# A transformer step on one core: the first mixture of experts gets its whole issue order written out, with all norms ahead, the gates of three chunks in one chain, and the rotary angles and the first attention block spread over the pairs

## The chip, the cores and the metric

The kernel runs on one core of one Trainium2 chip, as a single launch. The metric is the device time of that launch in microseconds. Before the change it is 1956.31 us, the median of three runs (1955.98 to 1956.78).

The core has five engines with a queue of instructions each: TensorE (PE) multiplies matrices, VectorE (DVE), ScalarE (ACT) and GpSimd (POOL) do the elementwise work, and SyncE (SP) issues the transfers between memory and the on-chip buffers. Every engine works its queue in order. Where an instruction waits for another engine, everything behind it on its own engine waits too.

## The reference

A batch of 2 sequences of 1024 tokens with 128 channels goes through six steps. The change touches the first and the beginning of the second:

```
x = x + 0.5 * L0_ffn(layernorm(x))        # mixture of experts: the "first mixture"
x = x + L0_attn(layernorm(x))             # attention, 16 heads of 64, over 1024 tokens
x = x + 0.5 * L0_ffn(layernorm(x))        # the same mixture again
x = x + 0.5 * L1_ffn(layernorm(x))        # two layers of local attention and gated MLP
x = x + L1_attn(layernorm(x))             # linear attention
x = x + 0.5 * L1_ffn(layernorm(x))

def L0_ffn(xf):                           # 16 experts of width 64, one shared expert of width 128
    shared = silu(xf @ Sg) * (xf @ Su) @ Sd
    probs  = softmax(xf @ Wr)             # 16 values for each token
    cw     = probs where it is one of the two largest, else 0
    routed = sum over e of cw[:, e] * (silu(xf @ Wg[e]) * (xf @ Wu[e]) @ Wd[e])
    return routed + shared

def L0_attn(x):
    q, k, v = heads of x @ qkv_w.T
    ang = pos[:, None] * rope_freqs       # q and k are rotated by cos(ang), sin(ang)
    scores = q @ k.T / 8 - p * log1p(a * abs(i - j))      # p, a: one number for each head
    return softmax(scores) @ v @ out_w.T
```

The routing is computed densely: every expert sees every token, and the weight `cw` sets most of the products to zero.

## The kernel before, in words

Everything is float32. `x` stays on chip as 16 tiles of 128 tokens by 128 channels. The kernel is built in Python; a loop in it is unrolled into instructions.

**The mixture** (`mixture`, L195) works on four chunks of 512 tokens. For each chunk there is a *front*. It has 13 parts (`front_parts`, L274): five for the norm (statistics on DVE, a negated mean on POOL, Ln and Exp on ACT, the offset on POOL, and four normalises on ACT, `norm_pieces`, L147), a transpose of four tiles on PE (`front_turned`), its copy by ACT (`front_kept`, into `xnT`), the logits on PE (`front_logits`), four parts for the gates (`front_gates`, L225: softmax and the two largest of 16, some twenty small operations on DVE and one Exp on ACT), and `front_weights` (L262), which transposes the weights on PE, copies them by DVE and stores them in DRAM.

After that come nine *pairs* for each chunk: first the shared expert (number `NP` = 8), then eight pairs of experts. A pair consists of

- `entered` (L294): the gate and up matmuls into one of two double banks of the accumulator memory,
- `fetched` (L303): two transfers of a row of weights from DRAM, repeated over 64 partitions (`cb`),
- `gated` (L310): silu on ACT; `multiplied` (L318): the product with `up` on DVE; `weighted` (L322): the product with `cb` on POOL (not for the shared expert),
- `left` (L326): the down matmuls, which add into `acc`. `finish` (L344) adds half of `acc` to `x`, on DVE.

**What is done beside the pairs.** `run_moe` (L350) walks over chunks and pairs and calls `prepare` (L455) after each pair. After the second pair of chunk 0 that emits `tables` (L413): the loads of the query and key weights and their scaling on POOL, the distances `dist`, and the rotary angles: sixteen DVE operations on 128x1024 that reduce the angle into the range of the sine, then Sin and Abs on ACT. In chunk 1 it emits the four bias pieces for the heads of pairs 0 and 1 (`bias_part`: Ln on ACT and a multiply on DVE, 128x1920). After chunk 1 and after chunk 3 it emits the attention's norm and transposes for one batch (`norm_transposed`, L177). In chunks 2 and 3 it emits the twelve *units* of the first attention block (`block_of`, L485): eight `rotary` units (one matmul each; two DVE products each; after every second one two POOL sums and eight small transfers into `qk`) and four `values` units.

**What sets the order.** In the first mixture the order in which Python emits is only a proposal: the framework's scheduler places the instructions of each engine by its own estimate. So the gate operations of chunk 1 stand between the angle operations on DVE, and the scores of the first attention step come ahead of the last down matmul on PE. In the attention (L657) and in the later stages the order is written out by hand (`tc.manual_schedule()`), and the queues hold what Python emits.

**The attention** runs 128 steps, one for each group of heads, batch, pair of heads and tile of 128 queries. Each takes scores (`scores_of`), the sum with the bias and its extremum on DVE (`maxima`, L558), Exp on ACT, a scaling on POOL, transposes, and, two to four steps later, the product with the values. The next block's units and the next pairs' bias pieces (L671 to L674) go beside the steps.

**Queues and buffers that the change touches.** SP issues all transfers in order, and a ninth waits for the completion of the first of the last eight. The double bank of `entered` has two buffers, `h` three, `cb` four, `xnT` two.

Of the kernel before, what the change touches and what calls it, by code (L numbers as in the profile page):

```python
# [8 lines left out]
F32 = mybir.dt.float32  # L9
# [22 lines left out]
def macaron_kernel(ctx: ExitStack, tc: tile.TileContext, a: dict, out: bass.AP):  # L32
# [41 lines left out]
    for i in range(4):  # L74
        nc.sync.dma_start(out=x[:, 4 * i : 4 * i + 4, :], in_=xv[:, 4 * i : 4 * i + 4, :])

    wr = keep.tile([P, E], F32, name="wr")
    nc.sync.dma_start(out=wr, in_=a["L0_ffn_Wr"])
# [6 lines left out]
    nc.sync.dma_start(out=wg, in_=a["L0_ffn_Wg"].rearrange("e p f -> p e f"))  # L85
    nc.sync.dma_start(out=wu, in_=a["L0_ffn_Wu"].rearrange("e p f -> p e f"))
    nc.sync.dma_start(out=wd, in_=a["L0_ffn_Wd"].rearrange("(i e) f m -> (e f) i m", e=2))
    nc.sync.dma_start(out=sg, in_=a["L0_ffn_Sg"])
    nc.sync.dma_start(out=su, in_=a["L0_ffn_Su"])
    nc.sync.dma_start(out=sd, in_=a["L0_ffn_Sd"])  # L90

# [23 lines left out]
    def norm_stats(src, n, name):  # L115

        st = small.tile([P, TB, 6], F32, tag="st", name=f"st_{name}")
        mv = small.tile([P, TB, 2], F32, tag="mv", name=f"mv_{name}")
        for i in range(n):
            nc.vector.bn_stats(st[:, i, :], src[:, i, :])  # L120
            nc.vector.bn_aggr(mv[:, i, :], st[:, i, :])
        rs = small.tile([P, TB], F32, tag="rs", name=f"rs_{name}")
        nc.scalar.activation(rs[:, :n], mv[:, :n, 1], AF.Ln, bias=eps)
        nc.scalar.activation(rs[:, :n], rs[:, :n], AF.Exp, scale=-0.5)
        nb = small.tile([P, TB], F32, tag="nb", name=f"nb_{name}")
        nc.gpsimd.tensor_scalar(nb[:, :n], mv[:, :n, 0], -1.0, 1.0, ALU.mult, ALU.mult)
        nc.gpsimd.tensor_tensor(nb[:, :n], nb[:, :n], rs[:, :n], ALU.mult)
        return rs, nb

# [8 lines left out]
    def log_and_exp(ins):  # L138

        with tc.issue_after(ins.ins):  # L140
            nc.scalar.preload_act_table_set("natural_log_exp_and_others")

    def normalise(dst, src, stats, k):
        rs, nb = stats
        nc.scalar.activation(dst, src, AF.Identity, bias=nb[:, k : k + 1], scale=rs[:, k : k + 1])

    def norm_pieces(src, n, name, dst):  # L147

        st = small.tile([P, TB, 6], F32, tag="st", name=f"st_{name}")
        mv = small.tile([P, TB, 2], F32, tag="mv", name=f"mv_{name}")  # L150
# [1431 lines left out]
```

## Time and profile before

| | us |
|---|---|
| median of 3 runs | 1956.31 |
| the profiled execution | 1957.24 |
| its span, first to last instruction | 1955.5 |
| PE busy in the span | 1841.8 (94%) |
| DVE, ACT, POOL busy | 1393.9, 1164.9, 1126.0 |
| first instruction of PE | 13.69 |
| first gate matmul of the mixture | 17.82 |
| end of the last down matmul of the first mixture | 164.72 |
| first score sum of attention step 2 on DVE | 183.39 |

The span and the busy times come from the page of the profile, the positions from the timeline of the instructions, counted from the first instruction. How the page is read: a group of the same instructions has one line, with the tile it writes, an arrow, the tiles it reads, their shapes, the count, the busy time and the mean of one; after the bar stands the idle time of that engine just before them, and who ended it. A matmul in float32 appears as two instructions. PE's granted clock is given as a share of full speed.

The first mixture and the ramp of the attention take the first tenth of the span. The rest (attention, second mixture, local and linear attention) runs with PE above 80% in every slice but the last.

### The profile page before, as it was taken

The numbers are of one execution on the slowest core, as the hardware profiler recorded it, in microseconds if no ns is written. First come the engines' busy times: TensorE is split into PE (matmuls) and PEld (weight loads), VectorE is DVE, ScalarE is ACT, GpSimd is POOL, SyncE is SP. The second block draws the span as 40 slices with busy tenths as digits, with TensorE's granted clock in tenths as the row PEclk, the third lists the DMA queues.
The fourth block names the chain that finished last, engine by engine and source line by source line (L and its number), as shares of the span: only waits on it lengthen the run. The fifth ranks groups of instructions, "written<-read, shape, count | busy, mean of one in ns | idle before, by whom it ended". The sixth has DMA issues, their size and how long they took to land.

```text
span 1955.5 us, 37604 instructions
## 1 busy us (share of the span) xinstructions
PE 1841.8 (94%) x14460; PEld 1176.5 (60%) x14460; DVE 1393.9 (71%) x2466; ACT 1164.9 (60%) x2132; POOL 1126.0 (58%) x1028
## 2 busy tenths in 40 slices
PE   4998999999999999999999988999999899999997
PEld 2554666656665665656566556666656466666665
DVE  6555767786777767776763468788877888887883
ACT  6344555665566555665655456776666566677674
POOL 2344434354444435344444379888877788788883
PEclk8998999999999999999999999999999999999999
DMA  5221101010000101012013211111100000011111
GB/s 134 76 80 41 34 1 34 12 31 14 22 23 12 33 12 34 2 32 70 1 67 89 74 28 29 25 24 25 26 18 15 6 18 18 20 26 23 26 32 27
DMA packets 52415, 64.15 MB, mean 33 GB/s; under 512 B 17890, under 2 KB 26892, under 8 KB 51980
## 3 DMA queue, kind: packets, MB, share of 16 engines
q1 hardware_dynamic: 52236, 61.74, 12.4%
q8 instruction: 115, 1.88, 0.4%
q14 instruction: 64, 0.52, 0.1%
HBM read 27.89 MB, written 1.31 MB: 15 GB/s over the span
## 4 chain that ended last, share of the span: by engine, by line
PE 62%; DVE 13%; ACT 10%; issue 7%; POOL 6%; SPq 1%; DMA 1%; DVEq 0%; POOLq 0%; ACTq 0%
PE s L549 11%; PE tp L599 10%; PE av L616 9%; PE qk_f L877 4%; ACT p L578 3%; PE pq L497 2%; PE av_f L1049 2%; PE gu_m L300 2%; PE gu_m L301 2%; PE tq_f L944 2%; PE s_f L988 2%; PE tp_f L1035 2%; PE pj_f L1065 2%; PE acc_m L284 2%; PE v_f L955 2%
## 5 line engine op out<-in xcount | busy, mean ns | idle before, releaser
L585 POOL TENSOR_SCALAR p<-p,den 128x1024 f32<-128x1024 f32 x256 | 291.9, 1153 | 396.5 <-DVE den L583 312.8
L578 ACT ACTIVATE p<-p,nm 128x1024 f32<-128x1024 f32 x256 | 294.7, 1151 | 364.7 <-DVE nm L565 348.4
L565 DVE CUSTOM_DVE_ANT_0 p<-s,bias 128x1024 f32<-128x1024 f32 x256 | 302.9, 1220 | 110.4 <-PE s L549 109.1
L599 PE MATMUL tp<-ident,p 128*128 128x128 f32 x2048 | 275.3, 277 | 13.5 <-ACT pt L603 12.7
L599 PEld LDWEIGHTS tp<-ident,p 128*128 128x128 f32 x2048 | 225.6, 141 | 100.8 <-ACT pt L603 37.5
L549 PE MATMUL s<-qk,qk 64*128 64x512 f32 x1024 | 257.8, 618 | 0.3 <-DVE nm L565 0.3
L616 PE MATMUL av<-pt,v 128*64 128x256 f32 x2048 | 249.0, 385 | 0.0
L605 DVE COPY pt<-tp 128x512 f32<-128x512 f32 x256 | 176.3, 689 | 93.9 <-PE tp L599 93.6
L616 PEld LDWEIGHTS av<-pt,v 128*64 128x64 f32 x2048 | 135.8, 136 | 150.1 <-issue 83.7
L923 POOL TENSOR_TENSOR t_f<-t_f,t_f 128x1024 f32<-128x1024 f32 x64 | 151.3, 2365 | 31.1 <-ACT vo_f L966 20.1
L324 POOL TENSOR_TENSOR h_m<-h_m,cb_m 128x512 f32<-128x512 f32 x64 | 81.8, 1282 | 124.8 <-DVE h_m L320 108.4
L603 ACT COPY pt<-tp 128x512 f32<-128x512 f32 x256 | 147.6, 577 | 5.9 <-PE tp L599 5.9
L549 PEld LDWEIGHTS s<-qk,qk 64*128 64x128 f32 x1024 | 89.1, 187 | 84.1 <-issue 81.5
L890 ACT ACTIVATE t_f<-qk_f 128x1024 f32<-128x1024 f32 x64 | 65.5, 1024 | 111.2 <-PE qk_f L877 103.0
L898 DVE TENSOR_TENSOR t_f<-qk_f,tab 128x1024 f32<-128x1024 f32 x64 | 78.3, 1224 | 74.1 <-ACT t_f L890 74.1
L1027 POOL TENSOR_TENSOR s_f<-s_f,sm_f 128x1024 f32<-128x1024 f32 x64 | 121.5, 1899 | 9.9 <-DVE sm_f L1023 9.8
L877 PE MATMUL qk_f<-wqkv,hT 128*128 128x512 f32 x256 | 121.7, 598 | 5.0 <-DVE hT L871 1.9
L1013 POOL TENSOR_TENSOR s_f<-s_f,mx_f 128x1024 f32<-128x1024 f32 x64 | 123.9, 1935 | 0.4 <-DVE mx_f L1008 0.4
L928 POOL TENSOR_TENSOR t_f<-t_f,rn_f 128x1024 f32<-128x1024 f32 x64 | 122.0, 1905 | 0.2
L320 DVE TENSOR_TENSOR h_m<-h_m,gu_m 128x512 f32<-128x512 f32 x72 | 49.2, 686 | 89.4 <-ACT h_m L316 89.2
L316 ACT ACTIVATE h_m<-gu_m 128x512 f32<-128x512 f32 x72 | 42.9, 597 | 115.5 <-PE gu_m L301 108.0
L513 POOL TENSOR_TENSOR rot<-rot,rot 128x512 f32<-128x512 f32 x32 | 40.7, 1273 | 88.1 <-DVE rot L508 88.1
(380 smaller groups left out, 3783.8 us busy)
## 6 DMA issues: line engine op xcount, KB each, us to landing
cb_m<-cwd_m SPq DMA_DIRECT2D x128, 128.0 KB, 3.0
qk<-rot SPq DMA_DIRECT2D x256, 64.0 KB, 2.0
tab<-in_xpos_dram SPq DMA_DIRECT2D x2, 1024.0 KB
wqkv<-in_L_ffn_wqkv_dram SPq DMA_DIRECT2D x2, 768.0 KB, 8.3
x<-in_L_attn_x_dram SPq DMA_DIRECT2D x4, 256.0 KB, 3.0
wraw<-in_qkv_wT_dram SPq DMA_DIRECT2D x2, 512.0 KB
vb_f<-vo_f SPq DMA_DIRECT2D x8, 128.0 KB, 2.5
out_dram<-x SPq DMA_DIRECT2D x4, 256.0 KB, 2.3
```

The costliest lines, as they stand in the source:

```text
L549: nc.tensor.matmul(pss[r][:, c, :], lhsT=qT[rows[r], t * P : (t + 1) * P], rhs=kT[rows[r], c * 512 : (c + 1) * 512], start=True, stop=True,)
L565: nc.vector.tensor_tensor_reduce(out=s, in0=pss[r].rearrange("p a n -> p (a n)"), in1=bias[r][:, o : o + S], scale=-1.0, scalar=3.0e38, op ...
L578: nc.scalar.activation(s, s, AF.Exp, bias=nm[:, r : r + 1], scale=-1.0, accum_out=den[:, r : r + 1])
L585: nc.gpsimd.tensor_scalar(probs[i, r], probs[i, r], den[:, r : r + 1], 1.0, ALU.mult, ALU.mult)
L599: nc.tensor.transpose(tp[:, k * P : (k + 1) * P], s[:, kb * P : (kb + 1) * P], ident)
L603: nc.scalar.copy(dst, src)
L605: nc.vector.tensor_copy(dst, src)
L616: nc.tensor.matmul(po[r * 64 : r * 64 + 64, 0 : 2 * P], lhsT=v[:, kb, r * 64 : r * 64 + 64], rhs=pts[i // 2, r, g][:, kb - 4 * g, :], star ...
L877: nc.tensor.matmul(ps[:, s, :], lhsT=hTs[b][:, n * P : (n + 1) * P], rhs=lw[l][0][:, s * INNER : (s + 1) * INNER], start=True, stop=True,)
L923: nc.gpsimd.tensor_tensor(t1, t1, t2, ALU.add)
L928: nc.gpsimd.tensor_tensor(t3, t3, rn.unsqueeze(2).to_broadcast([P, 2 * HL, 64]), ALU.mult)
L1013: nc.gpsimd.tensor_tensor(s3, s3, mx.unsqueeze(2).to_broadcast([P, HL, P]), ALU.subtract)
```

## The change

The scheduler no longer places the first mixture: `first_mixture` writes the order of all engines out.

- **Loads.** `x` still comes first, with `wr` behind its first quarter; then `sg`, `su`, `wg`, `wu`, `sd`, `wd`. The loads of `wv` and `wo` move from the start into slots 6 and 10, those of the query and key weights into slots 2 and 8 (a slot is one pair of one chunk, 36 in all).
- **Norms and gates.** The statistics of all 16 tiles are taken before the first pair; chunk 0 is normalised on ACT, chunks 1 to 3 on POOL from one Ln and one Exp. The logits of chunks 1 to 3 go into one bank, and their gates run as one chain on 12 tiles. `xnT` has four buffers, `cb` and `h` five.
- **Slots.** In slot s come `entered`, `gated`, `multiplied` and `weighted` of slot s, then `left` of slot s - 3, then what is listed beside the slot, then `fetched` of slot s + 3. Beside the slots: `front_weights` of chunks 1, 2, 3 at 4, 8, 12; one angle operation in each of the slots 4 to 19, computed in place in `sinT` and `cosT`; Abs and Sin at 20 and 21; batch 0's norm at 12, 21 and 22, with the normalises on DVE; the units of block 0 in slots 23 to 34; the bias of pair 0 in four halves at 35.
- **Activation tables.** They are switched explicitly (`log_exp_set`, `silu_set`).
- **Attention.** The norm of batch 1 is split: half of its statistics at slot 30, the rest and the first normalises at slot 38, the transposes at steps 0 and 1. The bias of pair 1 moves into steps 3, 4, 5 and 7.

```diff
-    for i in range(4):
-        nc.sync.dma_start(out=x[:, 4 * i : 4 * i + 4, :], in_=xv[:, 4 * i : 4 * i + 4, :])
...
+    for i in range(4):
+        nc.sync.dma_start(out=x[:, 4 * i : 4 * i + 4, :], in_=xv[:, 4 * i : 4 * i + 4, :])
+        if i == 0:
+            nc.sync.dma_start(out=wr, in_=a["L0_ffn_Wr"])
...
+    def silu_set():
+        if written[-1] != "silu":
+            nc.scalar.preload_act_table_set("silu_and_others")
+            written.append("silu")
...
-    def run_moe(name, beside):
...
-            def tables(mp):
...
+            def angles(mp):
+                ang, kk = sinT, cosT
...
+                def cosine():
+                    nc.scalar.activation(cosT, ang, AF.Abs)
+                    silu_set()
+                    nc.scalar.activation(cosT, cosT, AF.Sin, bias=halfpi, scale=-1.0)
+                def sine():
+                    silu_set()
+                    nc.scalar.activation(ang, ang, AF.Sin)
+                return ops, cosine, sine
+            def norm_of_batch(b):
...
+                mo, ne, ro, of_, ap = norm_pieces(src, TB, f"a0{b}", xas, nc.vector)
...
+            def first_mixture(mp):
+                LAG = 3
+                fronts, left, finish, front_parts, pair_parts = mixture("m0", mp, cbs=5, hs=5, cws=2, xts=4)
...
+                mo0, ne0, ro0, of0, ap0 = norm_pieces(x[:, 0:4, :], 4, "m00", x0)
+                mo1, ne1, ro1, of1, ap1 = norm_pieces(x[:, 4:NT, :], 12, "m01", x1, nc.gpsimd, mp)
+                for fn in (mo0, ne0, ro0, of0, mo1, ap0):
+                    fn()
+                fronts[0] = (x0,)
+                turned_(0)
+                for fn in (ne1, ro1, of1):
+                    fn()
+                kept(0)
+                logits(0)
...
+                apply1(1)
+                gates(0, 0)
+                gates(0, 1)
+                lg = bankO("lg_m01", 0).rearrange("p (t e) -> p t e", e=E)[:, :12, :]
+                for c in range(1, 4):
+                    fronts[c] = (x1[4 * c - 4 : 4 * c],)
+                    turned_(c)
+                    if c < 3:
+                        apply1(c + 1)
+                    kept(c)
+                    logits(c, lg, 4 * c - 4)
+                fronts[1] = lg
+                gates(0, 2)
+                gates(1, 0, 12)
+                gates(1, 1, 12)
+                gates(0, 3)
+                silu_set()
+                entered(*slots[0])
+                entered(*slots[1])
...
+                at(0, weights, 0)
+                for s in (1, 2):
+                    at(0, fetched, *slots[s])
+                at(0, gates, 1, 2, 12)
+                at(2, gates, 1, 3, 12)
+                for c, s in ((1, 4), (2, 8), (3, 12)):
+                    at(s, lambda c=c: weights(c, fronts[1][2], 4 * c - 4))
+                load, scaled = query_weights(mp)
+                for s, at_load, at_scale in ((0, 2, 7), (1, 8, 12)):
+                    at(at_load, load, s)
+                    for u in range(2):
+                        at(at_scale + u, scaled, s, u)
...
+                at(5, nc.scalar.activation, dist, dist, AF.Abs)
+                at(6, lambda: nc.sync.dma_start(out=wv, in_=qw[:, 2 * n : 3 * n]))
+                at(10, lambda: nc.sync.dma_start(out=wo, in_=a["out_wT"].rearrange("(j p) m -> p j m", p=P)))
+                for k, op in enumerate(ops):
+                    at(4 + k, op)
+                at(4 + len(ops), cosine)
+                at(5 + len(ops), sine)
+                mo, ne, ro, of_, ap, up = norm_of_batch(0)
+                at(12, mo, range(4))
+                at(21, mo, range(4, TB))
+                for fn in (ne, ro, of_, silu_set):
+                    at(21, fn)
+                at(22, ap, 0)
+                at(22, up, 0)
+                at(22, ap, 1)
+                at(23, up, 1)
+                for u in range(12):
+                    at(23 + u, lambda u=u: blocks[0][2].pop(6 - 2 * (u // 3) if u % 3 == 2 else 0)())
+                mo, ne, ro, of_, ap2, up2 = norm_of_batch(1)
+                at(30, mo, range(4))
+                at(35, log_exp_set)
+                for k in range(4):
+                    at(35, bias_part, 0, k // 2, slice(k % 2 * WIDE // 2, (k % 2 + 1) * WIDE // 2))
+                for fn, *more in ((mo, range(4, TB)), (ne,), (ro,), (of_,), (ap2, 0)):
+                    at(38, fn, *more)
+                for s in range(len(slots) + LAG):
+                    if s < len(slots):
+                        if s > 1:
+                            entered(*slots[s])
+                        gated(*slots[s])
+                        multiplied(*slots[s])
+                        if slots[s][1] < NP:
+                            weighted(*slots[s])
+                    if s >= LAG:
+                        left(*slots[s - LAG])
+                        if slots[s - LAG][1] == NP - 1:
+                            finish(slots[s - LAG][0])
+                    for fn in beside.pop(s, ()):
+                        fn()
+                    if s + 3 < len(slots) and slots[s + 3][1] < NP:
+                        fetched(*slots[s + 3])
+                return ap2, up2
...
-            run_moe("m0", prepare)
+            with ExitStack() as ms, tc.manual_schedule():
+                ap2, up2 = first_mixture(pool("moe_m0", 3, ms, side="right", reuse_waits="tile"))
...
-                            if (b, j) == js and t in places and (hg + 1 < H0 // 4 if b else hg > 0):
+                            if (b, j) == js and t in places and (hg + 1 < H0 // 4 or not b):
...
+                    elif i == 0:
+                        up2(0)
+                        ap2(1)
                     elif i < len(steps):
+                        if i == 1:
+                            up2(1)
```

Behind attention step 14 the order of every engine's work is the same as before.

## The prediction

> **What bounds the kernel now.** I read the summary first: TensorE (PE) is busy 94% of the span and is the bound nearly everywhere, so a change gains only where PE stands idle or runs slowly. The table of stages says where that is.
>
> ```profile
> 0.00:16.00 16.00, 1.64 (x4) 0.73 (x4) 3.33 (x24) 10.86 (x19) 3.73 (x19) 1.00 0.99 230
> 16.00:30.00 14.00, 13.56 (x48) 7.96 (x48) 7.53 (x26) 9.23 (x14) 3.21 (x5) 1.00 0.41 122
> 30.00:170.00 140.00, 113.39 (x508) 67.61 (x508) 78.96 (x174) 59.40 (x85) 53.14 (x46) 0.95 0.25 73
> ```
>
> Columns: window, length, then PE, weight load, VectorE (DVE), ScalarE (ACT), GpSimd (POOL) busy, granted PE clock, DMA share, GB/s. Before 16 us PE waits for loads and norms; from 30 to 170 it is idle 26.6 us, and the clock is not always full. The timeline of PE shows the rest.
>
> ```profile
> 17.82 2.06 PE L300 MATMUL gu_m<-xnT_m,sg 128*128 128x512 f32 x2
> ...
> 32.29 2.08 PE L300 MATMUL gu_m<-xnT_m,wg 128*128 128x512 f32 x2 [2.64 <-DVE h_m L320]
> ...
> 49.57 2.07 PE L300 MATMUL gu_m<-xnT_m,wg 128*128 128x512 f32 x2 [11.90 <-DVE h_m L320]
> ...
> 59.49 1.02 PE L300 MATMUL gu_m<-xnT_m,wg 128*128 128x512 f32 x2
> 60.35 1.02 PE L301 MATMUL gu_m<-xnT_m,wu 128*128 128x512 f32 x2
> 61.21 1.05 PE L284 MATMUL acc_m<-wd,h_m 128*128 128x128 f32 x8
> 62.10 1.02 PE L300 MATMUL gu_m<-xnT_m,wg 128*128 128x512 f32 x2
> ...
> 163.56 1.16 PE L284 MATMUL acc_m<-wd,h_m 128*128 128x128 f32 x8 [0.22 <-POOL h_m L324]
> ...
> 171.32 2.40 PE L188 MATMUL tp_a<-ident,xn_a 128*128 128x128 f32 x6 [5.54 <-ACT xn_a L145]
> ```
>
> By the starts, a warm pair costs 0.86 + 0.86 + 0.89 = 2.61 us of PE. After a gap of 2.64 us or more the same matmul takes 2.07 instead of 1.02: the clock has fallen. The 11.90 us gap has its cause on DVE, in its timeline:
>
> ```profile
> 43.36 0.69 DVE L445 TENSOR_SCALAR kk<-ang 128x1024 f32<-128x1024 f32 x1
> 44.10 0.68 DVE L446 TENSOR_SCALAR kk<-kk 128x1024 f32<-128x1024 f32 x1
> ...
> 45.57 1.22 DVE L449 SCALAR_TENSOR_TENSOR ang<-kk,ang 128x1024 f32<-128x1024 f32 x1
> ...
> 48.84 0.68 DVE L320 TENSOR_TENSOR h_m<-h_m,gu_m 128x512 f32<-128x512 f32 x1
> ```
>
> Sixteen angle operations and the gates of chunk 1 run as one block, and the product that PE waits for stands behind them. The chain of waits says the same: issue on DVE for 15.12 us at 34.44.
>
> **The change, part by part.** A slot is one pair of one chunk, 36 in all. I follow the changed issue order of each engine with durations of these rows.
>
> *The front moves ahead.* Loads: x0 stays first, so the first norm still starts at 3.81. The two iotas (1.73, 0.98) go ahead of POOL's first norm work, hidden by the wait for x (done near 4.4). Statistics 1.2, Ln 0.29, Exp 0.20, offset 0.20, four normalises of 0.40: 7.5. Then the new waits: ACT's copy of chunk 0 stands behind Ln and Exp of the other twelve tiles, which wait for x3 and 24 DVE statistics, about 9.3 (12 x 0.21 and 12 x 0.09). Ln, Exp 9.9; copy 0.56; cold logits 1.89: 12.4. Chunks 1 to 3 follow one by one on PE and ACT: transposes 0.9 cold (0.44 warm), copy with its waits 0.76, logits 1.89 (0.86 warm): 3.5 each cold, 2.1 warm. First gate matmul at 22.9 cold, 18.7 warm; I take 22.9, since the gaps keep recurring, against 17.82 before: 5.1 lost. POOL's twelve normalises are not in the trace: between 0.20 (128x8) and 1.15 (128x1024) each, near 0.3, so 3.6 us beside PE's 10.5; at 1.15 the last chunk comes near 24 and T (the first gate matmul) at about 27. The weight loads, of which sg and su now come ahead of wg and wu, are covered: the 3.2 MB up to wd need 14 us at 230 GB/s.
>
> *Fill.* The gates of chunk 0 end only after chunk 3's logits: two DVE operations on 12 tiles and eight small ones, T + 2.8. First product T + 5.2; weights transposed T + 6.1, copied T + 6.8. From the store of such weights (24.74) to the first POOL product (31.07) the trace has 6.3 us: T + 13.1, product 1.3 to 1.7, so the down matmul of slot 1 starts at T + 14.5. On the way DVE does the 12-tile gates, 16 operations on 192 elements, each between 0.22 (64) and 0.68 (512), near 0.35: 5.6 us so that the bank for slot 3's gate/up comes free only at T + 10.3, which PE feels as a gap of 2.6 and a cold restart. With down 0, gate/up 4 and down 1 behind it, down of slot 1 ends between T + 15.6 (warm) and T + 17.6 (cold); I take T + 17 = 40.
>
> *The slots.* From there PE has 31 gate/up of 1.72 (53.3), 34 downs of 0.89 (30.1), three weight transposes of 0.44, eight transposes (0.9) and twelve units of block 0 (10.4): 96.0 us. Do the others keep up? PE returns to a bank two slots later, 3.5 us after the gate/up that filled it; silu 0.60, product 0.69 and handovers take 1.6, and an angle operation between products costs 0.68 to 1.22 (1.64 once). POOL has 1.28 of 2.61; the down now stands three slots behind, so a late POOL product is covered for 5 us. SP: the rows are fetched three slots ahead (7.8 us) and land in 3.0; the moved loads of 0.5 MB (wraw, wv, wo) stand ahead of some fetches for about 2.2, and eight rotary DMAs for 5.6, both inside that lead and the down's. With these covers gone each would show as a wait of 1 to 3. I add 1.5 for small waits (0 to 6).
>
> One stall I can place, at slots 21 and 22. ACT has there silu, Abs 1.04, Sin 1.15, silu, Sin 1.06, a table load 1.28, Ln, Exp 0.5, a second load 1.28, and only then silu of slot 22: at 9.5 on a clock that starts with slot 20's gate/up, 2.6 after its matmuls. The product of slot 22 stands ahead of the normalises on DVE, and PE's transposes of batch 0 wait for those, from 7.8 to 11.2 on that clock: 3.4 idle plus about 1.7 of cold clock, 5 (bounds 1.5 and 6). Behind those transposes on PE stands gate/up of slot 23.
>
> The gap of 2.64 at 32.29 already ended cold, and my 1.7 rests on that row. The Trainium skill (TensorE: Matmul & The Clock Gate, Part 1) gives about 3.4 us of a free-running window before the clock falls; by it this gap might pass warm, the stall would be 3.3, and the result 1934.
>
> The table loads of the trace are 1283 ns, the next activation follows at once, and five remain of twenty up to 200 us. The Trainium skill (ScalarE: Activation LUTs, What ACT_TABLE_LOAD costs) puts 2.66 us on a switch, drain included. That speaks against two switches inside the pairs: the stall would be 7.8 and the result 1939. No drain shows between rows here.
>
> *End of the mixture*: 40 + 96.0 + 1.5 + 5 = 142.5 against 164.7.
>
> *Into attention.* Bias of pair 0 now comes after the last silu: table load 1.28, four half logarithms of 1.19 and DVE multiplies (0.75 to 1.66), then the residual: the first score sum starts 4.3 after the mixture instead of 1.8, and the last rotary DMAs may hold it to 5.2. Batch 1's norm is split around it; PE idles about 6 again and is cold. I get the first sum of step 2 at 19 after the mixture (15 to 22); before it is 183.39 - 164.72 = 18.7. So this gap is moved, not removed: 161.5.
>
> *Bias of pair 1* moves into steps 3, 4, 5, 7. Later groups carry such pieces: the gap between DVE sums is then 6.7 to 7.8 instead of 6.56, +0.8 over steps 35 to 39, up to +4 over 27 to 31. I take 1.5.
>
> Sum: 161.5 + 1.5 - 183.4 = -20.4. Behind attention step 14 the order of all engines is the same. Profiled execution 1957.24 (span 1955.5 and 1.74 around it), 0.93 above the median of the runs: 1956.31 - 20.4 = 1935.9, say **1936**.
>
> **The rivals.** (A) As above, 1929 to 1943.
>
> (B) More: PE warm through the logits (-4.2), slot 22 at its low bound (-3.5), step 2 at 16 (-3): 1925.
>
> (C) Less: the slots never run free. If DVE and POOL leave the 0.25 us that the pairs show before now (2.86 per pair from 58.49 to 72.78), 36 slots cost +7.5 more than my 1.5, and bias pieces +2.6: 1946.
>
> (D) Slower: the angle operations share the slots with POOL. In the trace L446 takes 1.64 us beside a POOL product and 0.68 alone. If product and angle operation each wait out a POOL product of 1.28, DVE needs 0.69 + 1.28 + 1.64 + 1.28 = 4.9 per slot against 2.61, over 16 slots +36.6: 1972. It decides from 3.9 us a slot. Against it: from 120 to 160 us the pairs before, with rotary work on DVE and POOL between them, keep PE 98% busy.
>
> (E) Nothing gained: the order is written but a serial piece (logits, fill, ramp) eats it, 1956. It needs T at 40 or more; no row gives that.
>
> **How the numbers follow.** A 0.56, B 0.15, C 0.21, D 0.06, E 0.02. About 0.2% (3.9 us) can be told from no change. The range goes from B to just over C: 1924 to 1947. Faster is A, B, C: 0.92; same 0.02; slower 0.06.
>
> **What would show it.** First gate matmul near 23, down of slot 1 near 39; no DVE wait over 4 us between 45 and 130 except one of 3 to 4 before the batch 0 transposes; last down near 142; five table loads; a PE gap of about 6 before batch 1's transposes; step 2's sum near 161. Wrong if slots cycle above 3 us without units, or if the first gate matmul comes after 28.

## The result, and the profile after

| | before | after |
|---|---|---|
| median of the runs side by side | 1956.55 us | 1934.11 us |
| ratio, 95% interval | | 0.988 [0.987, 0.990] |
| span of the profiled execution | 1955.5 | 1932.6 |
| first gate matmul | 17.82 | 22.59 |
| last down matmul of the mixture ends | 164.72 | 144.21 |
| first score sum of attention step 2 | 183.39 | 159.81 |

The forecast was 1936, with a range of 1924 to 1947. The table of stages of the changed kernel, with the same columns as before:

```profile
0.00:16.00 16.00, 6.59 (x26) 5.29 (x27) 6.87 (x42) 5.27 (x12) 9.70 (x30) 1.00 0.81 178
16.00:30.00 14.00, 12.60 (x40) 7.54 (x38) 4.72 (x16) 4.03 (x7) 0.00 (x0) 1.00 0.01 2
30.00:170.00 140.00, 125.65 (x563) 76.74 (x564) 89.69 (x172) 49.17 (x74) 72.11 (x56) 0.94 0.34 94
```

PE gains 5.0 us of work in the first 16 us (the logits of chunks 0 and 1 and the transposes of chunks 1 and 2) and 12.3 us between 30 and 170, where it now idles 14.35 us instead of 26.6. The timeline of PE has what is left of the waits ("warm" and "cold" below: the same pair of matmuls at about 1.02 and at up to 2.07 us). The clock's column is no witness for the start: it has 1.00 there, while the first gate pair at 22.59 took 2.06, for the record of the clock begins only at 25.7.

```profile
22.59 2.06 PE L275 MATMUL gu_m<-xnT_m,sg 128*128 128x512 f32 x2
...
32.47 2.07 PE L275 MATMUL gu_m<-xnT_m,wg 128*128 128x512 f32 x2 [2.52 <-DVE h_m L295]
...
38.59 1.05 PE L259 MATMUL acc_m<-wd,h_m 128*128 128x128 f32 x8
...
90.87 0.48 PE L422 MATMUL tp_a<-ident,xa 128*128 128x128 f32 x1 [2.93 <-DVE xa L132]
92.07 0.99 PE L422 MATMUL tp_a<-ident,xa 128*128 128x128 f32 x3 [0.73 <-DVE xa L132]
92.85 1.92 PE L275 MATMUL gu_m<-xnT_m,wg 128*128 128x512 f32 x2
...
141.82 2.39 PE L259 MATMUL acc_m<-wd,h_m 128*128 128x128 f32 x16 [0.88 <-POOL h_m L299]
150.76 1.24 PE L422 MATMUL tp_a<-ident,xa 128*128 128x128 f32 x4 [4.64 <-DVE xa L132]
```

The gap of 11.90 us is gone. From the down of slot 1 (38.59) to the end of the mixture PE waits three times: 2.93, 0.73 and 0.88. The angle operations that made the old gap now stand singly on DVE, one between two products, and the product waits for its silu, not for them, even behind the longest:

```profile
53.40 0.69 DVE L295 TENSOR_TENSOR h_m<-h_m,gu_m 128x512 f32<-128x512 f32 x1 [0.60 <-ACT h_m L291]
54.01 1.60 DVE L393 SCALAR_TENSOR_TENSOR sinT<-cosT,sinT 128x1024 f32<-128x1024 f32 x1
56.01 0.69 DVE L295 TENSOR_TENSOR h_m<-h_m,gu_m 128x512 f32<-128x512 f32 x1 [0.41 <-ACT h_m L291]
```

In the chain of waits, followed through the end of the mixture, the longest piece is no longer the 15.12 us of issue, but the bias of pair 0 on ACT:

```profile
139.86 1.28 ACT L120
141.16 4.43 ACT bias L561 x4
```

### The profile page after: what moved, and what is told of

It reads as the page before. It is cut to its first block, busy times and chain, and to the rows that moved or that the text cites. A ratio compares the mean times of both kernels' runs of the same rounds, so it can differ in the third digit from the quotient of the medians.

```text
span 1932.6 us, 37531 instructions
## 1 busy us (share of the span) xinstructions
PE 1836.6 (95%) x14460; PEld 1179.4 (61%) x14460; DVE 1395.0 (72%) x2450; ACT 1134.3 (59%) x2087; POOL 1137.8 (59%) x1036
## 4 chain that ended last, share of the span: by engine, by line
PE 65%; DVE 14%; ACT 10%; POOL 5%; issue 4%; DMA 0%; SPq 0%; DVEq 0%; ACTq 0%; POOLq 0%
PE s L630 10%; PE tp L680 10%; PE av L697 9%; PE qk_f L964 4%; ACT p L659 4%; PE gu_m L275 3%; PE gu_m L276 3%; PE acc_m L259 3%; PE pq L578 2%; PE tp_f L1122 2%; PE av_f L1136 2%; PE s_f L1075 2%; PE pj_f L1152 2%; DVE t_f L985 2%; PE tq_f L1031 2%
## 5 line engine op out<-in xcount | busy, mean ns | idle before, releaser
L680 PE MATMUL tp<-ident,p 128*128 128x128 f32 x2048 | 275.4, 277 | 14.4 <-ACT pt L684 13.6
L299 POOL TENSOR_TENSOR h_m<-h_m,cb_m 128x512 f32<-128x512 f32 x64 | 89.8, 1406 | 115.5 <-DVE h_m L295 75.8
```

The source lines that it names most:

```text
L680: nc.tensor.transpose(tp[:, k * P : (k + 1) * P], s[:, kb * P : (kb + 1) * P], ident)
```

## The experiments

Each kernel below is the changed kernel with one edit, unless the text says more. "Mixture ends" is the end of the last down matmul, "step 2" the first score sum of that step, both in the profiled execution. Ratios are to the kernel before on the same chip, so they, and not the medians, are to be compared between groups of runs; 0.001 is 2 us.

| edit | median us | ratio, 95% | first gate | mixture ends | step 2 |
|---|---|---|---|---|---|
| (the changed kernel) | 1934.1 | 0.9883 [0.9866, 0.9901] | 22.59 | 144.21 | 159.81 |
| angles in one block | 1947.7 | 0.9952 [0.9937, 0.9967] | 22.95 | 160.04 | 175.55 |
| lag 1 | 1948.5 | 0.9958 [0.9942, 0.9975] | 22.03 | 156.27 | 172.90 |
| lag 2 | 1936.7 | 0.9894 [0.9879, 0.9909] | 22.18 | 144.75 | 161.24 |
| fronts in slots | 1956.9 | 1.0000 [0.9991, 1.0010] | 10.64 | 168.48 | 183.91 |
| fronts in slots, spaced | 1946.4 | 0.9952 [0.9938, 0.9965] | 10.51 | 156.12 | 171.20 |
| transposes a slot later | 1938.3 | 0.9902 [0.9886, 0.9919] | 22.86 | 145.37 | 163.40 |
| weights of chunk 0 early | 1929.9 | 0.9871 [0.9858, 0.9885] | 23.08 | 140.42 | 156.00 |
| bias of pair 0 in the front | 1929.8 | 0.9875 [0.9862, 0.9889] | 21.93 | 143.01 | 154.96 |
| the last two together | 1928.8 | 0.9861 [0.9846, 0.9875] | 24.87 | 142.58 | 154.42 |
| and angles a slot sooner | 1932.4 | 0.9873 [0.9858, 0.9888] | 24.97 | 142.03 | 157.02 |
| all, and rows fetched sooner | 1920.0 | 0.9818 [0.9804, 0.9832] | 23.02 | 135.28 | 149.57 |

### The spreading of the angles

```diff
                 for k, op in enumerate(ops):
-                    at(4 + k, op)
+                    at(4, op)
```

> The sixteen angle operations stand as one block behind the product of slot 4 again; all else is the changed kernel. My theory, that spreading them is a large part of the gain: their rows of before add up to about 15 us of VectorE, the products of slots 5 and 6 stand behind them, PE is covered for some 3.5 us, so a gap of 10 to 13 us comes back near 45 us, with a cold restart: 1943 to 1950 against 1934.1, 1946 likeliest. Rival: the work is only as long as the lag of three downs and the looser banks allow, and the block is mostly hidden: within 3 us of 1934.

Measured 1947.7, 13.6 above. The gap that the change had removed is back (11.90 us before), and it is the only wait of PE between 40 and 66 us. PE first, then DVE:

```profile
58.85 2.07 PE L275 MATMUL gu_m<-xnT_m,wg 128*128 128x512 f32 x2 [12.53 <-DVE h_m L295]
```

```profile
45.24 7.53 DVE L393 SCALAR_TENSOR_TENSOR sinT<-cosT,sinT 128x1024 f32<-128x1024 f32 x6
...
58.11 0.68 DVE L295 TENSOR_TENSOR h_m<-h_m,gu_m 128x512 f32<-128x512 f32 x1
```

So neither the lag nor the deeper buffers hide a block of 16.5 us (41.74 to 58.19); the spreading does. The rival (within 3 us) falls.

### The lag of the down matmuls

```diff
-                LAG = 3
+                LAG = 1
...
-                    at(38, fn, *more)
+                    at(36, fn, *more)
```

> The down matmul stands one slot behind its gate/up instead of three. My theory, that the lag covers the chain silu 0.60, product 0.69, POOL product 1.28: with handovers some 2.9 us against the 1.72 of one gate/up, so PE waits 1.0 to 1.4 in each slot that has no rotary unit or transpose and less in the others: +25 to +40, 1959 to 1974, and every one of these waits shows as released by POOL. Rival: the order around the slots, not the lag, removed the small waits of before: within 4 us of 1934.

The lag counts, but 14.4 instead of 25 to 40. Between 40 and 160 us PE waits twelve times for POOL, 7.1 us in all; its other waits, 3.3 us, are those for the transposes at slot 22. The timeline of PE has:

```profile
71.22 1.16 PE L259 MATMUL acc_m<-wd,h_m 128*128 128x128 f32 x8 [1.31 <-POOL h_m L299]
...
77.23 1.16 PE L259 MATMUL acc_m<-wd,h_m 128*128 128x128 f32 x8 [0.36 <-POOL h_m L299]
```

From 46.22 to 96.34 the timeline has 16 slots and two weight transposes of 0.44: (50.12 - 0.88) / 16 = 3.08 a slot against 2.61, 0.47 lost. My sum had left out that with a lag of 1 the down of the slot before (0.89) still stands between a gate/up and its own down. The cover is 0.89 + 1.72 = 2.61 and the chain 2.9: 0.3 in a plain slot, as at 77.23 (0.36), and more in others: the POOL product ahead of 71.22 took 2.82 us instead of 1.28.

```diff
-                LAG = 3
+                LAG = 2
...
-                    at(38, fn, *more)
+                    at(37, fn, *more)
```

> The down matmul stands two slots behind. My theory: the cover is then 1.72 + 0.89 + 1.72 = 4.3 us against a chain of 2.9, so the plain slots stay without waits; only where DVE or POOL are late (angle operations of 0.7 to 1.6 us, weights scaled on POOL) a wait of up to 1 shows: 1933 to 1938. Rival: the third slot of lag is needed because DVE and POOL stretch each other's operations: 0.5 us a slot or more, 1945 or above.

Measured 1936.7, inside the range, and the mixture ends 0.5 later. Its interval overlaps that of the changed kernel: the runs show no loss from two slots of lag in the body; the wait of the last downs for POOL is 1.68 instead of 0.88.

### All norms ahead

The fronts of chunks 1 to 3 go back into the slots, one step a slot:

```diff
-                for fn in (mo0, ne0, ro0, of0, mo1, ap0):
+                for fn in (mo0, ne0, ro0, of0, ap0):
...
-                at(0, gates, 1, 2, 12)
-                at(2, gates, 1, 3, 12)
-                for c, s in ((1, 4), (2, 8), (3, 12)):
-                    at(s, lambda c=c: weights(c, fronts[1][2], 4 * c - 4))
+                for c, s in ((1, 0), (2, 8), (3, 15)):
+                    for k, (lo, hi) in enumerate(((0, 1), (1, 3), (3, 5), (5, 7), (7, 9), (9, 11), (11, 13))):
+                        for fn, *more in front_parts[lo:hi]:
+                            at(s + k, fn, c, *more)
+                        if k in (1, 5):
+                            at(s + k, silu_set)
```

> Only chunk 0 is normed ahead; norm, transposes, logits and gates of chunks 1 to 3 go one step a slot into slots 0 to 6, 8 to 14 and 15 to 21, ScalarE applies those norms, and the log set is loaded six times more, with six loads back. My theory: the first gate matmul comes 11 to 13 us sooner (near 10.5), the three fronts cost PE about 4 warm instead of 10.5 cold, and each of the six visits to the log set (two loads of 1.28 and 0.5 of work between two silus, against some 2 us of cover) stalls PE for 1 to 3 us with its cold restart: net -5 to +10, 1929 to 1944, 1938 likeliest. So the norms ahead are worth little by themselves. Rival, that they carry much of the gain: each visit stalls as slot 22 does, 6.9 us, and the sum is +25 or more, 1959.

Measured 1956.9: the first gate matmul did come 12 us sooner, and all of the gain was gone, far outside my range. PE's waits by cause, between 10 and 125 us (engine, line, whom it waited for, us in total, times, longest):

```profile
PE cw_m L248 <- DVE pr_m L238: 18.0, 3, 6.3
PE tp_m L187 <- ACT xn_m L134: 8.4, 3, 4.3
PE tp_a L422 <- DVE xa L132: 2.6, 2, 1.8
```

At the banks, where silu and product would hold it behind a visit to the log set, PE waited only 0.7 us. It waited where I had put its own steps: in the slot in which, or right behind which, the gates and normalises ran. That left it open whether fronts in slots or my spacing cost the time, so the same was run with PE's steps two slots behind:

```diff
+                    (1, {0: (0, 4), 1: (4, 5), 3: (5, 7), 4: (7, 9), 5: (9, 11), 6: (11, 12), 7: (12, 13)}),
+                    (2, {8: (0, 1), 9: (1, 3), 10: (3, 5), 12: (5, 7), 13: (7, 9), 14: (9, 11), 15: (11, 12), 16: (12, 13)}),
+                    (3, {15: (0, 1), 16: (1, 3), 17: (3, 5), 19: (5, 7), 20: (7, 9), 21: (9, 11), 22: (11, 12), 24: (12, 13)}),
```

> As the run with the fronts of chunks 1 to 3 in the slots, with the six visits to the log set kept, but each of PE's steps stands two slots behind the work that it needs (transposes behind the normalises, weights behind the gates). That run was at 1956.9, with waits of 5.95, 5.76 and 6.30 us before the transposed weights and 4.27, 2.05 and 2.06 before the transposes. My theory, that these waits are of my spacing and not of fronts in slots: 18 to 26 us of waits and some 6 of cold clock go, 1924 to 1938. Then norms ahead are not what the change gains by. Rival: the visits to the log set and the longer VectorE queue turn into waits at the banks, since a front in a slot shares its engines with silu and product: 1945 or above, and the norms ahead carry the gain.

Measured 1946.4: by the ratios the spacing was worth 9, and 13 remain to the changed kernel. My theory falls a second time. The waits became other waits (same view):

```profile
PE tp_a L422 <- DVE xa L132: 8.6, 1, 8.6
PE cw_m L248 <- DVE pr_m L238: 5.3, 2, 3.3
PE gu_m L275 <- DVE h_m L295: 4.2, 2, 3.3
PE acc_m L259 <- DVE x L308: 3.4, 1, 3.4
```

The largest begins with two visits to the log set in one slot; behind the product of slot 22 the gates of chunk 3 then stand ahead of the normalises on DVE (100.52 to 103.24). On ACT, between the silus of slots 21 and 22:

```profile
92.14 1.28 ACT L120 ACT_TABLE_LOAD   x1
...
93.70 1.28 ACT L126 ACT_TABLE_LOAD   x1
95.00 1.06 ACT L405 ACTIVATE sinT<-sinT 128x1024 f32<-128x1024 f32 x1
96.07 1.28 ACT L120 ACT_TABLE_LOAD   x1
...
97.93 1.28 ACT L126 ACT_TABLE_LOAD   x1
99.22 0.60 ACT L291 ACTIVATE h_m<-gu_m 128x512 f32<-128x512 f32 x1
```

So against these two placements norms ahead and one chain of gates save 13 and 23 us, though they cost 12 us at the first gate matmul. That no placement of the fronts in the slots would do better is not shown.

### The stall at slot 22

```diff
-                at(22, up, 0)
-                at(22, ap, 1)
-                at(23, up, 1)
+                at(23, up, 0)
+                at(23, ap, 1)
+                at(24, up, 1)
...
-                    at(23 + u, lambda u=u: blocks[0][2].pop(6 - 2 * (u // 3) if u % 3 == 2 else 0)())
+                    at(24 + u, lambda u=u: blocks[0][2].pop(6 - 2 * (u // 3) if u % 3 == 2 else 0)())
```

> The transposes of batch 0 stand one slot later (23 and 24 instead of 22 and 23), and the twelve units of block 0 one slot later with them; the norm itself stays. My theory, that the 2.93 + 0.73 us at the transposes and the cold clock behind them, 6.9 us in all, are nothing but an order that asks too soon: PE then has gate/up 23 and down 20 to do while VectorE normalises, the wait falls to under 1 us and the clock stays full: 1927 to 1930 against 1934.1. Rival: the stall comes from ScalarE's two table loads, which hold the silu of slot 22, so PE stops at the next bank instead, at the same price: 1933 to 1936; or the last rotary transfers, a slot later, hold the first scores and give the gain back there.

No gain: 1936.6 to 1938.9 in three runs, ratio 0.9909 (the profiled one took 6948.5 us and is left out). The same kernel again:

> The kernel of the run with the transposes of batch 0 one slot later again, for a trace: that run's profiled execution was disturbed, and its other times, 1936.6 to 1938.9, were no gain. Two readings: either the 3.7 us of waits are still there at another place near slots 22 to 25 (the bank of slot 22's product, or the transposes, whose normalises VectorE begins only behind that product), or they have gone and the mixture ends 4 to 6 us sooner, and the first scores wait as long for rotary transfers a slot later. By the first the last down ends near 144 as now; by the second near 139 with the sum of step 2 still near 160. I take the first for the larger part.

Measured 1938.3. The first reading, which I took, is wrong: of the waits at slot 22 1.2 us is left, and the clock stays full. The second is half right: the gain is given back, but still inside the mixture, at the last downs. (Behind it the ramp takes 18.0 us instead of 15.6; there the wait before batch 1's transposes is 6.24 instead of 4.64.) PE:

```profile
91.80 0.33 PE L422 MATMUL tp_a<-ident,xa 128*128 128x128 f32 x1 [0.32 <-DVE xa L132]
93.00 0.84 PE L422 MATMUL tp_a<-ident,xa 128*128 128x128 f32 x3 [0.87 <-DVE xa L132]
...
138.78 1.16 PE L259 MATMUL acc_m<-wd,h_m 128*128 128x128 f32 x8 [1.84 <-POOL h_m L299]
143.29 2.08 PE L259 MATMUL acc_m<-wd,h_m 128*128 128x128 f32 x8 [3.36 <-POOL h_m L299]
```

What POOL waited for is a row of the weights, and what that row waited for is SP, which issues eight rotary transfers ahead of it. POOL, then SP (duration of the whole group of issues):

```profile
137.46 1.26 POOL L299 TENSOR_TENSOR h_m<-h_m,cb_m 128x512 f32<-128x512 f32 x1 [5.60 <-DMA cb_m<-cwd_m]
```

```profile
128.20 5.56 SPq L599 DMA_DIRECT2D qk<-rot  x8
133.80 2.51 SPq L283 DMA_DIRECT2D cb_m<-cwd_m  x4
139.98 5.97 SPq L599 DMA_DIRECT2D qk<-rot  x8
```

The changed kernel has the same late rows (POOL waits 10.0 us for three of them between 40 and 150 us, the longest 5.4; here 20.6 us for five). My reading is that there the stall at slot 22 makes PE late enough not to feel them. Take the stall away, and they are next; the last experiment tests that.

### Fill and ramp

```diff
                     turned_(c)
+                    if c == 3:
+                        weights(0)
+                        for s in (1, 2):
+                            fetched(*slots[s])
...
                     logits(c, lg, 4 * c - 4)
+                    if c == 1:
+                        gates(0, 2)
+                        gates(0, 3)
```

> The gates of chunk 0 are finished behind chunk 1's logits, its weights transposed behind chunk 3's transposes, and the first two fetches issued there. My theory: the wait of 2.52 us at slot 3's bank and its cold restart come from VectorE, which does the gates of chunk 0 and of twelve tiles after the logits; with the former done 8 us sooner the fill shortens, the down of slot 1 ends 2 to 5 us sooner against 39.5: 1929 to 1932. Rival: the fill is bound by the path gate/up, silu, product, POOL product and the weight loads, not by the gates: within 1.5 us of 1934.

The wait of 2.52 at slot 3's bank falls to 0.63, and its restart is warm (1.13 for the matmul instead of 2.07); the down of slot 1 stands at 36.14 instead of 38.59, the mixture ends 3.8 sooner, step 2 too. By the ratios the gain is 0.0012, about 2 us, and the intervals overlap; the profiles' spans say 4.6 (1928.0). I take a gain of 2 to 5, which the times alone do not show.

```diff
+                def first_bias(c):
+                    if c == 1:
+                        nc.vector.tensor_scalar(pa, pa, 0.01, None, ALU.max)
+                        nc.vector.tensor_scalar(pa[:, 0, :], pa[:, 0, :], -1.0, None, ALU.mult)
+                        nc.scalar.activation(dist, dist, AF.Abs)
+                    for k in ((0,), (1, 2), (3,))[c - 1]:
+                        bias_part(0, k // 2, slice(k % 2 * WIDE // 2, (k % 2 + 1) * WIDE // 2))
...
                     logits(c, lg, 4 * c - 4)
+                    first_bias(c)
...
-                for k in range(4):
-                    at(35, bias_part, 0, k // 2, slice(k % 2 * WIDE // 2, (k % 2 + 1) * WIDE // 2))
```

> The distances' Abs, the two small operations on the bias' parameters and the four half pieces of pair 0's bias stand in the front, between the copies of chunks 1 to 3, where ScalarE idles 2.9 us at a time with the log set loaded; behind the last silu only the table load remains. My theory: ScalarE is free 4.4 us sooner at the ramp, batch 1's norm follows sooner, the wait of 4.64 us before its transposes falls to 1 to 3 and the sums of step 2 and later come 2 to 4 us sooner: 1930 to 1932. Rival: the ramp is bound by VectorE's statistics, the residual and the maxima, so nothing moves: within 1 us of 1934; the front could also lose up to 2 us if a half piece delays a copy.

Step 2 comes 4.85 sooner, of which 3.65 is the ramp: from the mixture's end to step 2 it takes 11.95 instead of 15.6. (The other 1.2 lie ahead: the first gate matmul is 0.66 sooner, and slot 3's pair is faster behind the same wait of 2.52.) The wait of 4.64 is now

```profile
146.29 1.09 PE L422 MATMUL tp_a<-ident,xa 128*128 128x128 f32 x4 [1.36 <-DVE xa L132]
148.20 3.12 PE L634 MATMUL s<-qk,qk 64*128 64x512 f32 x8 [0.81 <-DVE nm L650]
```

That answers what the chain of waits had said of the bias: 4.43 of it lay on the path, and 3.65 come back in the ramp when it goes. (By the ratios the whole gain is 0.0008, 1.6 us, within the intervals; by the span 4.8.)

Both edits together, with the gates ahead of the bias pieces:

```diff
                     logits(c, lg, 4 * c - 4)
+                    if c == 1:
+                        gates(0, 2)
+                        gates(0, 3)
+                    first_bias(c)
```

> The weights of chunk 0 early and the bias of pair 0 in the front, together. They act at the two ends of the mixture, so their gains (4.6 and 4.8 us of span in the profiles, about 3 by the medians) should add: 1925 to 1929 at a before of 1956, ratio 0.984 to 0.986. Rival: both lay more on VectorE and ScalarE of the same 10 us of front, the gates of twelve tiles and their Exp come later for the bias pieces, and one of the gains is lost: 1930 or above, ratio 0.987.

Measured 1928.8, ratio 0.9861, in my range of times and just outside that of ratios. By the ratios the gains add (0.0022 against 0.0012 and 0.0008), but these differences are smaller than the intervals; by the profiles they add only in part: the span is 5.6 shorter instead of 9.4, and step 2 is 5.4 sooner instead of 8.7. A part of what is missing stands in the front. The bias parameters had come behind the gates on DVE, ACT waited for them, and the copy of chunk 2 and its logits behind that (ACT, then PE):

```profile
17.93 1.19 ACT L567 ACTIVATE bias<-dist,one,pa 128x960 f32<-128x960 f32 x1 [2.14 <-DVE pa L464]
```

```profile
19.64 1.89 PE L198 MATMUL lg_m<-wr,xnT_m 128*128 128x16 f32 x8 [2.68 <-ACT xnT_m L192]
```

This round of logits takes 5.5 us instead of 3.5.

On top of these two:

```diff
-                    at(4 + k, op)
-                at(4 + len(ops), cosine)
-                at(5 + len(ops), sine)
+                    at(3 + k, op)
+                at(3 + len(ops), cosine)
+                at(4 + len(ops), sine)
```

> As the two together, and all angle operations one slot sooner, from slot 3, so that the sine stands at slot 20 and ScalarE's queue in slot 21 holds the visit to the log set alone. Theory: silu of slot 22 comes 1 us sooner (the sine's 1.06), its product and the normalises too, and the stall before the transposes falls from 3.7 to 2.7 us of wait: 0.5 to 1.5 below the two together. Rival: VectorE has the gates of twelve tiles until slot 3, the first angle operation delays a product there, and a wait of 0.5 to 1 comes back: no difference within 0.5.

The stall fell as expected (2.49 + 0.88) and the mixture ended 0.55 sooner, yet the kernel was 2 to 4 us slower than the two together. In the profiles the difference is in the ramp, and it is the clock: behind the same two waits, 1.36 and 0.81, the score matmuls of step 1 take

```profile
147.22 4.32 PE L636 MATMUL s<-qk,qk 64*128 64x512 f32 x8 [0.81 <-DVE nm L652]
```

instead of 3.12, and the granted clock is 0.51 from 150 to 156 us where the other kernel has 1.00. That the edit causes this is not shown: one of the four executions of the two together took 1933.6 at a granted clock of 0.992, the other three 1928.0 to 1928.9 at 0.995; the four with the angles a slot sooner have 0.992 and 0.993.

### What the pieces give together

The two edits of the front, the transposes a slot later, and:

```diff
-                fronts, left, finish, front_parts, pair_parts = mixture("m0", mp, cbs=5, hs=5, cws=2, xts=4)
+                fronts, left, finish, front_parts, pair_parts = mixture("m0", mp, cbs=6, hs=5, cws=2, xts=4)
...
                     if c == 1:
                         gates(0, 2)
+                        nc.vector.tensor_scalar(pa, pa, 0.01, None, ALU.max)
+                        nc.vector.tensor_scalar(pa[:, 0, :], pa[:, 0, :], -1.0, None, ALU.mult)
+                        nc.scalar.activation(dist, dist, AF.Abs)
                         gates(0, 3)
...
-                    if s + 3 < len(slots) and slots[s + 3][1] < NP:
-                        fetched(*slots[s + 3])
...
+                    if s + 4 < len(slots) and slots[s + 4][1] < NP:
+                        fetched(*slots[s + 4])
                     for fn in beside.pop(s, ()):
                         fn()
```

> Weights of chunk 0 early, bias of pair 0 in the front (its parameters' two small operations now ahead of the last gates, since ScalarE waited 2.14 us for them and PE 2.0 longer for a copy), transposes of batch 0 one slot later, and the rows of the weights fetched four slots ahead, in front of the unit's transfers of the same slot, with six buffers for five. Theory: the transposes one slot later do free PE at slot 22 (the wait was 0.32 + 0.87 and warm), and what took the gain back is the row fetch: SyncE issues the eight rotary transfers for 5.57 us, the last fetches stand behind them, POOL waits 5.6 us for a row and the last downs 1.84 and 3.36 us for POOL. With the fetches ahead these two waits go, and the gains add: 2.0 from the copy and 3 to 5 from the stall, on the 1928.8 of the two together: 1921 to 1925. Rival: the first scores then wait for the last rotary transfers all the same, since these are issued behind POOL's last rotary product, and nothing but the 2.0 is gained: 1926 to 1928; or the late downs are POOL's own order (two rotary products ahead of the last product), and the wait of 3.4 us stays.

Measured 1920.0, ratio 0.9818 [0.9804, 0.9832]: clear of the changed kernel's interval, and 1 below my range. Against the kernel with the transposes a slot later alone, POOL's waits for rows fall from 20.6 to 7.5 us between 40 and 150 us, the last downs show no wait, and the mixture ends at 135.28:

```profile
88.37 0.33 PE L422 MATMUL tp_a<-ident,xa 128*128 128x128 f32 x1 [0.33 <-DVE xa L132]
...
132.44 2.84 PE L259 MATMUL acc_m<-wd,h_m 128*128 128x128 f32 x24
...
138.56 1.10 PE L422 MATMUL tp_a<-ident,xa 128*128 128x128 f32 x4 [1.36 <-DVE xa L132]
140.47 4.92 PE L635 MATMUL s<-qk,qk 64*128 64x512 f32 x8 [0.81 <-DVE nm L651]
```

The rival (first scores held by the rotary transfers) falls too: the first score matmuls start at 135.22, right behind the last down. How much of the gain over the two together each of the three added edits brings was not run apart. The profiled execution is that of 1925.3; the cold scores in its last line suggest why it is above the median. The other executions have no trace, but their granted clocks fit: 1919.7 to 1920.0 at 0.996, and 1924.5 and 1925.3 at 0.992.

## Why the prediction was right, point by point

- **First gate matmul**, 22.9: 22.59. The rounds of logits are 3.50 apart, all cold. POOL's normalises, bounded between 0.2 and 1.15, take 0.44 and are hidden.
- **Fill**, down of slot 1 ends at 40: 39.5, where the next instruction starts. The gap is 2.52 (2.6 forecast) and ended cold.
- **The gap that the change removes**: the prediction read 15.12 us of the chain of waits as DVE's issue. That row names no engine; it lies between two POOL products, and POOL's timeline of the kernel before has the wait for DVE's product there:

```profile
49.59 2.50 POOL L324 TENSOR_TENSOR h_m<-h_m,cb_m 128x512 f32<-128x512 f32 x2 [15.16 <-DVE h_m L320]
```

  The conclusion, that the product stands behind the angle block on DVE, rests on DVE's timeline and holds.
- **The slots**, 96.0 + 1.5 (34 downs of 0.89 are 30.3, not 30.1): from 39.5 to 144.2 there are 104.7; without the stall 97.8. The rival in which the slots keep 0.25 each is excluded by 40.00 us of PE busy between 100 and 140. The rival of DVE and POOL slowing each other is seen in single operations (a k_m product of 0.36 took 1.33); in the slots of the angles PE waits for none of them, but at slot 22 it does.
- **The stall at slot 22**, 5, at most 6: 6.9. The place and the chain on ACT were as forecast; the size was not. The matmuls behind it and its four cold groups start at 98.12; without waits and at full clock they would start at 91.26. Of the 6.9 between, 3.66 is waits (3.4 forecast) and 3.2 cold clock (1.7 forecast). The second wait was missing from my sum: POOL's product of slot 22 ran beside the normalises, and one of these took 1.29 us instead of 0.34 (POOL, then DVE):

```profile
90.63 1.30 POOL L299 TENSOR_TENSOR h_m<-h_m,cb_m 128x512 f32<-128x512 f32 x1 [2.36 <-DVE h_m L295]
```

```profile
90.73 1.29 DVE L132 TENSOR_SCALAR xa<-x,rs_a,nb_a 128x128 f32<-128x128 f32 x1
```

  The Trainium skill (SBUF — State Buffer, "SBUF: two separate sides") describes a port pair that whichever of VectorE and GpSimd starts first holds for its whole instruction, the other blocked; 1.29 beside a product of 1.30 agrees.
- **The clock after a gap**: by the Trainium skill (TensorE: Matmul & The Clock Gate, Part 1) the stall might have passed warm and the result been 1934, which is what was measured. That is chance: the matmul behind the stall took 1.92, so it was cold, as the row before had said, and the 2 us came from the ramp.
- **The table loads**: the Trainium skill (ScalarE: Activation LUTs, What ACT_TABLE_LOAD costs) has 2.66 us for a switch. In slot 21 the two loads, Ln and Exp together take 3.15 (86.09 to 89.24); a load is 1.28 and the next activation starts 0.02 later, so the price taken from the rows held.
- **End of the mixture**, 142.5: 144.2, the stall's surplus.
- **The ramp**, 19 (15 to 22): 15.6. This is the term that was mis-sized most. Table load, four half logarithms, the last multiply and the residual add up to 7.5 in the prediction's own rows (1.28, four of 1.19, 0.75, 0.68), so a first score sum at 4.3 lets the load begin some 3 us before the mixture ends. It begins at 139.86, 4.35 before the end, and the four halves at 141.16; the chain takes 7.0, and the first score sum comes 2.64 behind the end. That is 1.7 of the 3.4. The gap before batch 1's transposes is 4.64 (about 6 forecast), another 1.4.
- **Bias of pair 1**, 1.5: the lead over before is 23.6 at step 2 and 21.8 at step 7, so 1.8.

The likeliest case held; of the case with more gain only the ramp came true (its 16 against 15.6), and the logits were cold and the stall at slot 22 large, against it. The sum was -20.4. Measured are -22.9 on the span and -22.4 by the medians: +1.7 at the end of the mixture, -3.4 in the ramp, +0.3 from the bias, and -1.1 far behind the change: the lead stays at 21.8 to 21.9 from attention step 15 to step 127, and the rest arises behind 1015 us, where the order is the same. There the granted clock falls to half for 3.41 us at four places up to 1900 us in the profiled execution before, and at two after. So part of the closeness is luck: the surplus of the stall and the shorter ramp offset each other by half.

What the experiments add is the price of each part taken back alone: 13.6 for the spreading of the angles, 14.4 for two of the three slots of lag, 13 to 23 for the norms ahead. They sum to 41 and more, not to 22, so the parts are not independent and the gain cannot be divided among them; which covers for which was not tried. One thing follows: an order written out by hand gains nothing as such, for with the angles spread and the lag kept, but the fronts in the slots, the ratio was 1.0000 in one placement and 0.9952 in the other.

## What to carry to other kernels

Work that has no deadline inside a pipelined loop can be free when it is cut into pieces that fit beside one step: the same sixteen operations cost 12.5 us of idle matrix engine as a block of 16.5, and nothing one by one, in pieces of at most 1.60 beside a step of 2.61. Sizes between were not tried. Before a stall is removed, look for the queue that is late just behind it; here a transfer queue with eight issues of 5.6 us ahead of the next row stood behind the stall, and the gain was given back until the rows were asked for a step sooner and ahead of these issues. When work is moved off the end of a stage, start its clock at its own last input, not at the end of the stage.

## What was not expected of the hardware

Equal waits do not give an equal clock. The same wait of 2.52 us at slot 3's bank left the next pair of matmuls at 2.07 us in the changed kernel, at 1.39 and 1.40 in two others (transposes a slot later, angles in one block), and at 1.13, warm, in a fourth (bias of pair 0 in the front).

In the traces PE's granted clock stays at 1.00 or 0.50 for whole multiples of 3.41 us, and the edges of these stretches lie otherwise in each execution. Two stretches around that wait, in the changed kernel:

```profile
29.08:32.49 3.41, 0.89 (x4) 0.07 (x2) 3.17 (x10) 0.60 (x1) 0.00 (x0) 1.00 0.13 41
32.49:35.90 3.41, 3.41 (x4) 1.47 (x5) 3.20 (x8) 0.00 (x0) 1.63 (x2) 0.50 0.71 194
```

The whole wait lies in one stretch, and the next has half clock; so it is in the kernels with 1.39 and 1.40, where the edge comes a little later. With the bias in the front the wait is split over two, 0.57 and 1.95, and the clock stays full:

```profile
27.86:31.28 3.42, 2.85 (x10) 1.04 (x8) 2.11 (x6) 1.13 (x2) 0.00 (x0) 1.00 0.04 10
31.28:34.69 3.41, 1.46 (x4) 0.75 (x5) 3.24 (x9) 0.07 (x1) 0.00 (x0) 1.00 0.35 116
34.69:38.10 3.41, 3.41 (x18) 2.21 (x17) 3.24 (x6) 0.84 (x2) 2.69 (x2) 1.00 0.73 205
```

The Trainium skill (TensorE: Matmul & The Clock Gate, Part 1) has a window of this length that runs freely, not from the gap's start, which agrees; but it asks for a whole idle window, and here 2.52 us of idleness in one were enough.

That is not the whole rule. The two waits of 1.36 and 0.81 us in the ramp, with four transposes between them, left PE at full clock in two kernels (3.12 us for eight score matmuls) and slowed it in two others (4.32 and 4.92). With 4.92 both fall into one stretch (1.83 us idle). But with 4.32 they lie as with 3.12, 1.36 in one stretch and 0.83 in the next. What decides there was not tried.
